# Making W' by Strassen over halves of in, rank and out, in blocks of 128 rows of in

## The chip, the cores and the metric

The kernel runs on one core of a Trainium2 chip. The metric is the device time of one execution in microseconds (us). The engines of the core are called as the profile calls them: PE (TensorE, matrix products), PEld (its weight loads), DVE (VectorE), ACT (ScalarE), POOL (GpSimd) and SP (SyncE, which here only issues DMAs). Each engine works through its own queue of instructions in order, and the engines wait for one another by semaphores.

## The reference, cut to what matters

All numbers are float32. The input x is 32 samples of 128 x 2048. The program has two layers, each of them a mixing of channels and a product:

```python
# layer 0
agg_w, agg_b = softmax(mlp(cond)) @ weight, ... @ bias_k   # a 128x128 kernel for each sample
c   = einsum('boi,bih->boh', agg_w, x) + agg_b
out = einsum('bsd,od->bso', c, W) + bias                   # W: 2048 x 2048
xa  = einsum('bsd,erd->ebsr', c, A)                        # A: 16 x 16 x 2048
upd = einsum('ebsr,eor,e->bso', xa, Bf, coeffs * scales)   # Bf: 16 x 2048 x 16
x   = x + out + upd
# layer 1
c   = conv1d(x, 9 taps, 4 groups) + context + bias
x   = x + per_head_ffn(c)                                  # 16 heads of 128 -> 512 (gelu) -> 128
```

What matters here is that `out + upd` is one product with W' = W + Bf (w A), a matrix of 2048 x 2048 (in by out, as it is kept) whose second term is of rank 16 x 16 = 256. The change concerns how that second term is computed and added, and how W' is cut into blocks.

## The kernel before

**The product with W'.** The mixing of channels is linear and is done on the other side, so the product is x times W', over 4096 rows, 2048 in and 2048 out. It is done by Strassen's scheme (in Winograd's form, with seven products) over halves of rows, in and out. The seven outer products are the `ROUNDS`, in the order P1, P2, P6, P7, P5, P3, P4. Each round goes through eight groups g of rows, so there are 56 steps. A step is one call of `multiply` (L265), which is again Strassen's scheme with seven inner products P1 to P7, each of four 128x512 matmuls. The left operands are combinations of a tile of x, made by `x_combine` (L222) on POOL; the right operands are combinations of four quarters of a half-by-half piece of W', made by `inner_weights` (L184). POOL also makes the outer combinations of x (`x_outer`, L245, lines 249 and 251), for rounds to come, and stores them (L209). Each product goes to a PSUM bank, from which ACT copies it (L276) or DVE adds it (L274) into the output tile. There are eight banks, handed out and given back in a first-in, first-out list (`bank`, `done`). SBUF has 24 large slots of 8 KB a partition (`slot`).

**Making W'.** W' has 16 blocks. In the kernel before a block is (kh, oh, ki, oi): a half kh of in and a half oh of out, and halves ki and oi within these; it holds 512 rows of in (as four pieces kc of 128) and 512 columns of out. `w_load` (L151) loads W's block, and `w_make` (L156) adds the low-rank part: for each kc two matmuls (rank is 2 x 128) into a bank (L165), an add by DVE onto the loaded block (L169), and at the end a store into HBM (L171), since later rounds read the blocks again. A and Bf lie in SBUF in two halves each (`a_sb`, `bf_sb`), loaded by `low_load` (L130) on SP, and A is scaled by coeffs x scales on DVE (`a_scale`, L134). The first four blocks are made before step 0, since they are the right operand of round P1. The other twelve are made two at a time ahead of each of steps 0 to 5 ("pairs" 0 to 5 here). The first round's inner weights are made on DVE (line 869); those of the other rounds are made on POOL (lines 188, 189, 193 and 194).

**Row sums.** The sum of W' over in is needed for a bias. `row_sums` (L173) reduces a block's four pieces by a tensor_reduce on DVE (lines 178 and 181) and adds the result to `wsum` (L179).

**Order.** `tc.manual_schedule()` keeps the order of the program, so an instruction's place in its engine's queue is the place where it is written. The main part (from L785) issues the loads on SP, then the four first blocks, then the steps. In a step, operands and loads of the step that follows come first, then the making of the two blocks, then `multiply`, and `between(j)` puts other work after the j-th inner product. PE's waits follow from banks (a bank is written again only when it was read), operands, and accumulation: a product that adds to a bank comes after the read of what the bank held.

Of the kernel before, what the change touches and what calls it, by code (L numbers as in the profile page):

```python
# [8 lines left out]
FP = mybir.dt.float32  # L9
# [7 lines left out]
P = 128  # L17
# [34 lines left out]
def adaln_ffn_kernel(  # L52
# [29 lines left out]
    def bank():  # L82
        return banks.pop(0)
# [4 lines left out]
    def scratch(name, shape=(P, L)):  # L88
        return dram.tile(list(shape), FP, name=name, tag=name)
# [3 lines left out]
    wb_d = {  # L93
        (kh, oh, ki, oi): scratch(f"wb_d{kh}{oh}{ki}{oi}")
        for kh in range(2) for oh in range(2) for ki in range(2) for oi in range(2)
    }
    t2_d = {(ki, oi): scratch(f"t2_d{ki}{oi}") for ki in range(2) for oi in range(2)}
    w1_d = scratch("w1_d")
# [23 lines left out]

    a_sb = [slot(f"a_sb{h}", (P, 2, L // 2)) for h in range(2)]
    bf_sb = [slot(f"bf_sb{h}", (P, 2, L // 2)) for h in range(2)]

    def low(ts, c, i0, n):
        h, i0 = divmod(i0, L // 2)
        return ts[h][:, c, i0 : i0 + n]

    def low_load(ts, src, i0, n):  # L130
        h, j0 = divmod(i0, L // 2)
        nc.sync.dma_start(ts[h][:, :, j0 : j0 + n], src[:, :, i0 : i0 + n])

    def a_scale(i0, n):  # L134
        for c in range(2):
            cols = low(a_sb, c, i0, n)
            nc.vector.tensor_scalar(cols, cols, wsc[:, c : c + 1], None, ALU.mult)

# [8 lines left out]

    wsum = slot("wsum", (P, NPH, QW))
    seen = set()

    def w_load(kh, oh, ki, oi):  # L151
        t = slot(f"w_{kh}{oh}{ki}{oi}", (P, 4, QW))
        nc.sync.dma_start(t.rearrange("p k o -> p (k o)"), WT[kh, oh, ki, oi])
        return t

    def w_make(t, kh, oh, ki, oi):  # L156
        o = 2 * oh + oi
        for kc in range(4):
            pw = bank()
            i0 = kh * 1024 + ki * 512 + kc * P  # L160

            n = QW // 2 if i0 == 0 and o == 0 else QW
            for o0 in range(0, QW, n):
                for c in range(2):
                    nc.tensor.matmul(  # L165
                        pw[:, o0 : o0 + n], lhsT=low(a_sb, c, i0, P),
                        rhs=low(bf_sb, c, o * QW + o0, n), start=(c == 0), stop=(c == 1),
                    )
            nc.vector.tensor_tensor(t[:, kc], pw, t[:, kc], ALU.add)  # L169
            done(pw)  # L170
        nc.gpsimd.dma_start(wb_d[kh, oh, ki, oi], t.rearrange("p k o -> p (k o)"))  # L171

    def row_sums(t, oh, oi):  # L173
        o = 2 * oh + oi
        ks = t.rearrange("p k o -> p o k")
        if o in seen:
            part = agp.tile([P, QW], FP, name=f"part_{len(seen)}", tag="cq", bufs=1)
            nc.vector.tensor_reduce(part, ks, AX.X, ALU.add)
            nc.vector.tensor_tensor(wsum[:, o], wsum[:, o], part, ALU.add)  # L179
        else:  # L180
            nc.vector.tensor_reduce(wsum[:, o], ks, AX.X, ALU.add)
        seen.add(o)

    def inner_weights(name, t, eng=nc.gpsimd):  # L184

        b11, b12, b21, b22 = (t[k] for k in ((0, 0), (0, 1), (1, 0), (1, 1)))
        t1, t2, t4 = (slot(f"{name}_t{k}", (P, 4, QW)) for k in (1, 2, 4))
        eng.tensor_tensor(t1, b12, b11, ALU.subtract)
        eng.tensor_tensor(t2, b22, t1, ALU.subtract)
        if eng is nc.vector:  # L190
            t["late"] = b12
        else:
            eng.tensor_tensor(b12, b22, b12, ALU.subtract)
        eng.tensor_tensor(t4, b21, t2, ALU.subtract)
        return {"P1": b11, "P2": b21, "P3": b22, "P4": t4, "P5": t1, "P6": t2, "P7": b12}

# [68 lines left out]
    def multiply(r, g, lhs, rhs, olds, between):  # L265
# [13 lines left out]
        def product(k, ps, first, last):  # L279
            for kc in range(4):  # L280
                nc.tensor.matmul(  # L281
                    ps, lhsT=lhs[k][:, bass.ts(kc, P)], rhs=rhs[k][:, kc],
                    start=first and kc == 0, stop=last and kc == 3, skip_group_check=True,
                )
# [26 lines left out]

    def outer_weights(r, ki, oi):

        def get(d):
            t = slot(f"wo_{r}{ki}{oi}", (P, 4, QW))
            nc.sync.dma_start(t.rearrange("p k o -> p (k o)"), d)
            return t

        def w(kh, oh):
            return wb_d[kh, oh, ki, oi]  # L320

        tt = nc.gpsimd.tensor_tensor
        srcs = {
            "P6": [w(1, 1), w(0, 1), w(0, 0)],
            "P7": [w(1, 1), w(0, 1)],
            "P5": [w(0, 1), w(0, 0)],
            "P4": [w(1, 0), t2_d[ki, oi]],
            "P3": [w(1, 1)],
        }[r]
        ts = [get(d) for d in srcs]  # L330

        def combine():
            if len(ts) > 1:
                tt(ts[0], ts[0], ts[1], ALU.subtract)
            if len(ts) > 2:
                tt(ts[0], ts[0], ts[2], ALU.add)
                nc.gpsimd.dma_start(t2_d[ki, oi], ts[0].rearrange("p k o -> p (k o)"))
            return ts[0]

        return combine  # L340
# [325 lines left out]
    def small():  # L666
# [81 lines left out]
        for o in range(NPH):  # L748
            p5 = bank()
            for half in (slice(0, NQ), slice(NQ, QW)):  # L750
                nc.tensor.matmul(
                    p5[:, half], lhsT=ones, rhs=wsum[:, o, half], start=True, stop=True
                )
            nc.scalar.copy(wbc[:, o], p5)
            done(p5)
# [31 lines left out]
    blocks = [  # L787
        (kh, oh, ki, oi)
        for kh, oh in ((0, 0), (0, 1), (1, 1), (1, 0)) for ki in range(2) for oi in range(2)
    ]  # L790
    first = {}
    warm_up()
    nc.sync.dma_start(cs, coeffs)
    low_load(a_sb, A, 0, P)
    low_load(bf_sb, BfT, 0, QW // 2)
    low_load(bf_sb, BfT, QW // 2, QW // 2)
    nc.vector.tensor_tensor(wsc, cs[:, 0:2], cs[:, 2:4], ALU.mult)
    a_scale(0, P)
    low_load(a_sb, A, P, QW - P)
    a_scale(P, QW - P)  # L800
    low_load(bf_sb, BfT, QW, QW)
    wt = {k: w_load(*k) for k in blocks[0:1]}
    wt[blocks[1]] = w_load(*blocks[1])
    low_load(a_sb, A, QW, QW)
    xs = {0: [x_load(0, 0, 0)]}
    for k in blocks[2:4]:
        wt[k] = w_load(*k)

    def make(k):
        t = wt.pop(k)  # L810
        w_make(t, *k)
        made.append(k)
        if len(made) > 4:
            row_sums(t, k[1], k[3])
        return t

    steps = [(r, g) for r in ROUNDS for g in range(NG)]
    for i0 in (1024, 1536):
        low_load(bf_sb, BfT, i0, QW)
    for k in blocks[4:6]:  # L820
        wt[k] = w_load(*k)
    for i0 in (1024, 1536):
        low_load(a_sb, A, i0, QW)
    xs[0] += [x_load(0, 1, 0), x_load(0, 1, 1)]
    lhs = {}
    for n, k in enumerate(blocks[0:4]):
        first[k[2:]] = make(k)
        if n == 0:
            a_scale(QW, QW)
        if n == 1:  # L830
            lhs[0] = x_combine(*steps[0], xs.pop(0))
    rhs = inner_weights("P1", first, nc.vector)
    for i0 in (1024, 1536):
        a_scale(i0, QW)
    unsummed = [(0, 0), (1, 0), (1, 1)]
    olds = {}
# [8 lines left out]
    for i, (r, g) in enumerate(steps):  # L845
# [14 lines left out]
        if g == NG - 1 and 0 < ri < len(ROUNDS) - 1:  # L860
            nxt = inner_weights(ROUNDS[ri + 1], nxt)

        if ri == 0:
            for k in blocks[4 + 2 * g : 6 + 2 * g]:
                t = make(k)
                if "late" in first:
                    b12 = first.pop("late")
                    row_sums(b12, 0, 1)
                    nc.vector.tensor_tensor(b12, first[1, 1], b12, ALU.subtract)
                if k[:2] == (1, 0):  # L870
                    nxt[k[2:]] = t
        elif ri + 1 < len(ROUNDS):
            for k, combine in waiting.items():
                nxt[k] = combine()
            waiting = {}
            if 2 <= g < 6:
                k = ((g - 2) // 2, (g - 2) % 2)
                waiting[k] = outer_weights(ROUNDS[ri + 1], *k)

# [10 lines left out]
        def between(j):  # L890
# [3 lines left out]
            if ri == 0 and j == 2:  # L894
                for k in blocks[6 + 2 * g : 8 + 2 * g]:
                    wt[k] = w_load(*k)
            if ri == 0 and j == 4 and unsummed:
                ki, oi = unsummed.pop(0)
                row_sums(first[ki, oi], 0, oi)
            if last_round:  # L900
# [17 lines left out]
        if g == NG - 1 and ri + 1 < len(ROUNDS):  # L918
            rhs = nxt if ri > 0 else inner_weights(ROUNDS[ri + 1], nxt)
            nxt = {}  # L920
# [84 lines left out]
```

## Time and profile before

| What | us |
|---|---|
| median of three runs | 2664.43 (2660.68 to 2664.87) |
| the profiled execution | 2658.77 |
| its span on the core | 2657.0 |
| PE busy | 2630.5 |
| DVE busy | 1369.3 |
| POOL busy | 1087.3 |
| ACT busy | 535.2 |
| pair 0 on PE | up to 49.62 |
| step 0 on PE | 49.62 to 73.66 |
| a pair later on (32 PE instructions) | 13.81 |
| a step later on (56 PE instructions) | 24.03 |
| POOL's first inner weights for round P2 begin | 310.98 |

In the profile's rows a group of instructions is named by its line, engine and operation, then the tile that is written and the tiles that are read, by the names in the program, then its shape and count. A timeline's row has the start and the length in us ahead of that, and behind it in brackets how long the engine had been idle before and what ended the idle time. A 128x512 matmul in float32 is two PE instructions. PE's ends are modelled, and consecutive rows can overlap by a fraction of a us.

### The profile page before, as it was taken

What the parts mean: (1) busy time and instruction counts of PE and PEld (TensorE: products, weight loads), DVE (VectorE), ACT (ScalarE), POOL (GpSimd) and SP (SyncE); (2) the same over time, 40 slices, a digit from 0 to 9 for tenths busy, and PEclk for the clock granted to TensorE, in tenths of its full rate; (3) what the DMA queues carried; (4) which work ended last, traced back from release to release, by engine and by line L of the source; (5) the groups of instructions that cost most, each with busy time, mean ns of one, the idle gap of its engine ahead of it and who ended that gap; (6) DMA issues with size and microseconds to landing.
All of it is one profiled execution on the core that took longest, in us unless ns stands there. A gap on an engine that the chain in (4) does not pass through costs nothing.

```text
span 2657.0 us, 19770 instructions
## 1 busy us (share of the span) xinstructions
PE 2630.5 (99%) x6504; PEld 1235.7 (47%) x6504; DVE 1369.3 (52%) x2132; ACT 535.2 (20%) x1103; POOL 1087.3 (41%) x665
## 2 busy tenths in 40 slices
PE   9999999999999999999999999999999999999998
PEld 4444444444444444444444455554445544455543
DVE  6645245233344355444366667666666666666610
ACT  0000100000000000000011144434444444444432
POOL 3544645523646422656232233343333333343222
PEclk9999999999999999999999999999999999999999
DMA  8875548455366457555666788777788777777532
GB/s 332 349 303 232 233 170 328 158 199 201 155 265 239 157 238 285 221 217 210 219 235 204 249 298 285 229 219 239 232 248 248 225 229 226 239 244 232 164 124 87
DMA packets 183333, 609.14 MB, mean 229 GB/s; under 512 B 16832, under 2 KB 87488, under 8 KB 138816
## 3 DMA queue, kind: packets, MB, share of 16 engines
q1 hardware_dynamic: 148656, 466.40, 49.7%
q0 software_dynamic: 34144, 140.53, 15.4%
q8 instruction: 52, 0.85, 0.1%
q10 hardware_dynamic: 432, 0.96, 0.1%
q14 instruction: 49, 0.40, 0.0%
HBM read 364.03 MB, written 210.24 MB: 216 GB/s over the span
## 4 chain that ended last, share of the span: by engine, by line
PE 91%; DVE 4%; DMA 3%; POOL 1%; issue 1%; SPq 0%; POOLq 0%; ACT 0%; DVEq 0%; ACTq 0%
PE bank L281 47%; PE bank L626 16%; PE bank L637 16%; PE bank L484 6%; PE bank L394 4%; PE bank L165 2%; DVE ags L356 2%; DMA bf_sb<-in_BfT 1%; DMA xt<-in_xT 1%; DVE va L464 0%; DVE vb L463 0%; DMA wb_d<-w 0%; DVE u L274 0%; DMA ws<-in_ffw 0%; DVE vb L466 0%
## 5 line engine op out<-in xcount | busy, mean ns | idle before, releaser
L626 PE MATMUL bank<-t,ws 128*128 128x512 f32 x1024 | 460.4, 592 | 0.5 <-DMA ws<-in_ffw 0.5
L637 PE MATMUL bank<-gl,ws 128*128 128x512 f32 x1024 | 460.2, 592 | 0.0
L629 ACT ACTIVATE gl<-bank 128x512 f32<-128x512 f32 x512 | 306.1, 598 | 446.6 <-PE bank L626 430.1
L281 PE MATMUL bank<-P_t,s_P 128*128 128x512 f32 x896 | 393.8, 592 | 1.3 <-ACT m_P L276 0.9
L274 DVE TENSOR_TENSOR u<-bank,u 128x512 f32<-128x512 f32 x280 | 187.3, 687 | 398.3 <-PE bank L281 389.2
L644 POOL DMA_INDIRECT out<-t,orow x128 | 152.2, 1189 | 564.5 <-DVE t L642 503.2
L637 PEld LDWEIGHTS bank<-gl,ws 128*128 128x128 f32 x1024 | 194.6, 190 | 233.0 <-issue 231.0
L626 PEld LDWEIGHTS bank<-t,ws 128*128 128x128 f32 x1024 | 194.4, 190 | 227.5 <-issue 219.7
L281 PE MATMUL bank<-wo_P,s_P 128*128 128x512 f32 x640 | 284.7, 596 | 4.4 <-DVE u L274 4.4
L281 PEld LDWEIGHTS bank<-P_t,s_P 128*128 128x128 f32 x896 | 170.1, 190 | 215.3 <-issue 214.8
L385 ACT ACTIVATE bank<-w,aggb 128x512 f32<-128x512 f32 x128 | 80.8, 684 | 892.2 <-DMA w<-w_d 874.1
L642 DVE TENSOR_TENSOR t<-bank,t 128x512 f32<-128x512 f32 x128 | 87.9, 687 | 319.0 <-PE bank L637 304.8
L377 POOL TENSOR_TENSOR x<-x,fb 128x1024 f32<-128x1024 f32 x64 | 155.9, 2454 | 228.3 <-DMA x<-in_x 150.5
L274 DVE TENSOR_TENSOR p<-bank,p 128x512 f32<-128x512 f32 x112 | 77.3, 690 | 241.7 <-PE bank L281 241.7
L281 PEld LDWEIGHTS bank<-wo_P,s_P 128*128 128x128 f32 x640 | 121.5, 191 | 159.6 <-issue 149.5
L356 DVE SCALAR_TENSOR_TENSOR ags<-mix,att_bc,ags 128x128 f32<-128x128 f32 x224 | 174.5, 779 | 4.5
L281 PE MATMUL bank<-wo_P,xt 128*128 128x512 f32 x384 | 169.0, 592 | 0.0
L610 POOL DMA_INDIRECT t<-hx_d,row x128 | 125.0, 977 | 55.5 <-issue 25.0
L232 POOL TENSOR_TENSOR s_P<-xt 128x512 f32<-128x512 f32 x40 | 52.2, 1306 | 229.5 <-DMA xt<-in_xT 221.7
L281 PE MATMUL bank<-P_t,xt 128*128 128x512 f32 x320 | 144.0, 592 | 0.1
L484 PE MATMUL bank<-va,tw_l 128*128 128x256 f32 x512 | 123.0, 381 | 7.3 <-DVE va L467 7.1
L484 PEld LDWEIGHTS bank<-va,tw_l 128*128 128x128 f32 x512 | 96.7, 190 | 50.1 <-issue 38.0
(136 smaller groups left out, 2811.2 us busy)
## 6 DMA issues: line engine op xcount, KB each, us to landing
xt<-in_xT SPq DMA_DIRECT2D x64, 1024.0 KB
u<-u_d SPq DMA_DIRECT2D x40, 1024.0 KB
wo_P<-wb_d SPq DMA_DIRECT2D x36, 1024.0 KB
u<-c_d SPq DMA_DIRECT2D x64, 512.0 KB
x<-in_x SPq DMA_DIRECT2D x32, 1024.0 KB
xg<-x SPq DMA_DIRECT2D x256, 128.0 KB
hx_d<-x1t SPq DMA_DIRECT2D x32, 1024.0 KB
hx_d<-ht SPq DMA_DIRECT2D x32, 1024.0 KB
```

The source lines that it names most:

```text
L274: nc.vector.tensor_tensor(to, ps, to, ALU.add)
L281: nc.tensor.matmul(ps, lhsT=lhs[k][:, bass.ts(kc, P)], rhs=rhs[k][:, kc], start=first and kc == 0, stop=last and kc == 3, skip_group_check ...
L356: nc.vector.scalar_tensor_tensor(ag, mix[:, k], att, ag, ALU.mult, ALU.add)
L377: nc.gpsimd.tensor_tensor(xt[:, f : f + 2], xt[:, f : f + 2], late["fb"][:, f : f + 2], ALU.add)
L394: nc.tensor.matmul(pm, lhsT=ag, rhs=u[:, f], start=False, stop=True, skip_group_check=True)
L484: nc.tensor.matmul(out, lhsT=w[:, 2 * i + r], rhs=rhs, start=first and r == 0, stop=last and r == 1, skip_group_check=True,)
L610: nc.gpsimd.indirect_dma_start(out=t.rearrange("p k t -> p (k t)"), out_offset=None, in_=hx_d[g].rearrange("l k t -> l (k t)"), in_offset= ...
L626: nc.tensor.matmul(pu, lhsT=w[:, m * P : (m + 1) * P], rhs=t[:, 0], start=True, stop=True)
L629: nc.scalar.activation(gl[m], pu, AF.Gelu)
L637: nc.tensor.matmul(pd, lhsT=w[:, (MC + m) * P : (MC + m + 1) * P], rhs=gl[m], start=(m == 0), stop=(m == MC - 1),)
L642: nc.vector.tensor_tensor(t[:, 1], pd, t[:, 1], ALU.add)
L644: nc.gpsimd.indirect_dma_start(out=out, out_offset=bass.IndirectOffsetOnAxis(ap=orow[:, g, h : h + 1], axis=0), in_=t[:, 1], in_offset=None,)
```

## The change

A block of W' becomes (kh, oh, kc): 128 rows of each half ki of a half of in, and both halves oi of a half of out; its tile is 128 x (ki, oi, 512). A block thus has all four quarters that Strassen's scheme combines, for 128 of 512 rows. The host lays out W accordingly.

- The first four blocks are made as before, by eight matmuls each (`w_make`). The inner weights of the first round are made for each of them as soon as it is there, 512 columns at a time, on DVE.
- The other twelve are made in pairs by the new `w_make_two`: the low-rank product is done by Strassen's scheme over halves of in (ki), rank (c) and out (oi), with seven matmuls a block. Each matmul accumulates into one of three banks of the block, and after each DVE adds the bank onto a quarter of the block. The combined operands come from `a_combine` and `b_combine`, and take four slots more.
- A's second half is loaded on SP behind the x tiles of step 0, by `a_load`, which also does the two scales on DVE; on DVE they stand behind `tb[1]`'s four subtractions and ahead of the adds of pair 0.
- `row_sums` is two adds of 128x1024 a block, after the first and the third inner product of a step; the first four blocks have theirs in step 0 behind pair 0 (one half) and after the fifth inner product of steps 0 to 3. `wsum` begins at zero.
- The inner weights of the later rounds are made on POOL in 16 pieces of 128x512 instead of four of 128x2048.

The diff, cut to its core:

```diff
-    def low_load(ts, src, i0, n):
-        h, j0 = divmod(i0, L // 2)
-        nc.sync.dma_start(ts[h][:, :, j0 : j0 + n], src[:, :, i0 : i0 + n])
-
-    def a_scale(i0, n):
+    def a_load(h, k0, k1):
+        for ki in range(2):
+            i0 = (2 * h + ki) * QW
+            nc.sync.dma_start(
+                a_sb[h][:, :, ki, k0:k1].rearrange("p c k i -> p c (k i)"),
+                A[:, :, i0 + k0 * P : i0 + k1 * P],
+            )
         for c in range(2):
-            cols = low(a_sb, c, i0, n)
+            cols = a_sb[h][:, c, :, k0:k1]
             nc.vector.tensor_scalar(cols, cols, wsc[:, c : c + 1], None, ALU.mult)
...
+    def a_combine(kh, tt):
+        s = slot(f"sa_{kh}", (P, 4, 4, P))
+        x11, x12, x21, x22 = (a_sb[kh][:, c, ki] for ki in range(2) for c in range(2))
+        tt(s[:, 0], x21, x22, ALU.add)
+        tt(s[:, 1], s[:, 0], x11, ALU.subtract)
+        tt(s[:, 2], x11, x21, ALU.subtract)
+        tt(s[:, 3], x12, s[:, 1], ALU.subtract)
...
+    def w_make_two(ks, ts, sa, tb):
+        pxs, pys, pzs = ([bank() for _ in ks] for _ in range(3))
+
+        def product(n, ps, first, last, ki, oi):
+            for (_, _, kc), p, t in zip(ks, ps, ts):
+                nc.tensor.matmul(
+                    p, lhsT=sa[n][:, kc], rhs=tb[n], start=first, stop=last, skip_group_check=True
+                )
+                nc.vector.tensor_tensor(t[:, ki, oi], p, t[:, ki, oi], ALU.add)
+
+        product("P1", pxs, True, False, 0, 0)
+        product("P2", pzs, True, True, 0, 0)
+        done(*pzs)
+        product("P6", pxs, False, False, 0, 1)
+        product("P5", pys, True, False, 1, 1)
+        product("P7", pxs, False, False, 1, 1)
+        product("P3", pys, False, True, 0, 1)
+        done(*pys)
+        product("P4", pxs, False, True, 1, 0)
+        done(*pxs)
...
-            nc.vector.tensor_reduce(part, ks, AX.X, ALU.add)
-            nc.vector.tensor_tensor(wsum[:, o], wsum[:, o], part, ALU.add)
...
+    def row_sums(oh, t):
+        for ki in range(2):
+            nc.vector.tensor_tensor(wsum[:, oh], wsum[:, oh], t[:, ki], ALU.add)
...
-        eng.tensor_tensor(t1, b12, b11, ALU.subtract)
-        eng.tensor_tensor(t2, b22, t1, ALU.subtract)
...
+        for kc, t in enumerate(ts):
+            b11, b12, b21, b22 = (t[:, ki, oi] for ki in range(2) for oi in range(2))
+            tt(t1[:, kc], b12, b11, ALU.subtract)
+            tt(t2[:, kc], b22, t1[:, kc], ALU.subtract)
+            tt(b12, b22, b12, ALU.subtract)
+            tt(t4[:, kc], b21, t2[:, kc], ALU.subtract)
...
+    a_load(0, 0, 1)
+    b_load(0, 0, 0, QW // 2)
+    b_load(0, 0, QW // 2, QW // 2)
+    b_load(0, 1)
+    a_load(0, 1, 4)
+    wt = {k: w_load(*k) for k in blocks[0:2]}
     xs = {0: [x_load(0, 0, 0)]}
     for k in blocks[2:4]:
         wt[k] = w_load(*k)
...
-    for i0 in (1024, 1536):
-        low_load(bf_sb, BfT, i0, QW)
+    for q in range(2):
+        b_load(1, q)
     for k in blocks[4:6]:
         wt[k] = w_load(*k)
-    for i0 in (1024, 1536):
-        low_load(a_sb, A, i0, QW)
     xs[0] += [x_load(0, 1, 0), x_load(0, 1, 1)]
...
+    for kc, t in enumerate(first):
+        k = blocks[kc]
+        w_make(k, t)
...
+        tt(t1[:, kc], t[:, 0, 1], t[:, 0, 0], ALU.subtract)
+        tt(t2[:, kc], t[:, 1, 1], t1[:, kc], ALU.subtract)
+        tt(t4[:, kc], t[:, 1, 0], t2[:, kc], ALU.subtract)
+    rhs = weights(first, t1, t2, t4)
+    tb[1] = b_combine(1, nc.vector.tensor_tensor)
+    a_load(1, 0, 4)
...
+                w_make_two(ks, two, sa[ks[0][0]], tb[ks[0][1]])
+                made.extend(ks)
+                if g == 0:
+                    for kc, t in enumerate(first):
+                        b12 = t[:, 0, 1]
+                        nc.vector.tensor_tensor(wsum[:, 0, 1], wsum[:, 0, 1], b12, ALU.add)
+                        nc.vector.tensor_tensor(b12, t[:, 1, 1], b12, ALU.subtract)
+                if g == 1:
+                    sa[1] = a_combine(1, nc.gpsimd.tensor_tensor)
+                if g == 3:
+                    tb[0] = b_combine(0, nc.gpsimd.tensor_tensor)
...
+            if ri == 0 and j in (1, 3) and unsummed:
+                row_sums(*unsummed.pop())
+            if ri == 0 and j == 5 and unsummed_first:
+                t = unsummed_first.pop(0)
+                tt = nc.vector.tensor_tensor
+                tt(wsum[:, 0, 0], wsum[:, 0, 0], t[:, 0, 0], ALU.add)
+                tt(wsum[:, 0], wsum[:, 0], t[:, 1], ALU.add)
```

`b_combine` does for Bf, over rank and out, what `a_combine` does for A.

## The prediction

> **What bounds the kernel now.** I read the busy times first: the time of this kernel is TensorE's time.
>
> ```profile
> span 2657.0 us, 19770 instructions
> PE 2630.5 (99%) x6504; PEld 1235.7 (47%) x6504; DVE 1369.3 (52%) x2132; ACT 535.2 (20%) x1103; POOL 1087.3 (41%) x665
> ```
>
> A matmul taken away saves its whole length, and a wait put on PE costs its whole length. The profiled execution took 2658.77 us, 5.66 below the median of the runs, 2664.43; I sum against the former and add 5.66 at the end. Next, PE's waits and the chain of waits in the stretch that the change touches:
>
> ```profile
> PE bank L145 <- DVE warm L142: 1.5, 1, 1.5
> PE bank L281 <- ACT m_P L276: 0.9, 1, 0.9
> PE bank L165 <- DMA bf_sb<-in_BfT: 0.8, 1, 0.8
> ```
>
> ```profile
> 112.84 13.81 PE bank L165 x32
> 126.66 24.03 PE bank L281 x56
> ```
>
> After the start PE waits once, 0.9 us, in the first 250 us. The chain alternates: 32 PE instructions for a pair of W' blocks, 13.81 us; 56 for a step, 24.03. A 128x512 matmul is two PE instructions, 13.81/16 = 0.86 us each.
>
> Then the timelines. Weight loads show PE's pace at the start:
>
> ```profile
> 2.48 0.34 PEld L145 LDWEIGHTS bank<-warm 128*128 128x128 f32 x1 [0.52 <-issue]
> 3.33 0.34 PEld L145 LDWEIGHTS bank<-warm 128*128 128x128 f32 x1 [0.52 <-issue]
> ...
> 11.00 0.19 PEld L165 LDWEIGHTS bank<-bf_sb,a_sb 128*128 128x128 f32 x1 [0.24 <-issue]
> 11.43 0.19 PEld L165 LDWEIGHTS bank<-bf_sb,a_sb 128*128 128x128 f32 x1 [0.24 <-issue]
> ```
>
> Start to start is 0.85 us cold and 0.43 later: PE begins at half pace. VectorE around pair 0 (PE: 35.9 to 49.62):
>
> ```profile
> 44.75 0.88 DVE L137 TENSOR_SCALAR a_sb<-a_sb,wsc 128x512 f32<-128x512 f32 x2 [1.12 <-DMA a_sb<-in_A]
> 46.06 0.88 DVE L137 TENSOR_SCALAR a_sb<-a_sb,wsc 128x512 f32<-128x512 f32 x2 [0.43 <-DMA a_sb<-in_A]
> 46.86 2.48 DVE L169 TENSOR_TENSOR w<-bank,w 128x512 f32<-128x512 f32 x4
> 49.37 7.36 DVE L181 TENSOR_REDUCE wsum<-w 128x512 f32<-128x2048 f32 x2
> 56.77 2.81 DVE L869 TENSOR_TENSOR w<-w,w 128x2048 f32<-128x2048 f32 x1
> ```
>
> The second half of A is scaled, as it lands, ahead of pair 0's adds in VectorE's queue. So those adds start at 46.86, 11 us after their matmuls did. PE did not notice: pair 0 needs eight banks, eight are there, and no matmul waits for an add. GpSimd gives the pace of the loads and a price of sharing:
>
> ```profile
> 53.58 1.27 POOL L232 TENSOR_TENSOR s_P<-xt 128x512 f32<-128x512 f32 x1 [15.96 <-DMA xt<-in_xT]
> ...
> 57.38 3.33 POOL L235 TENSOR_TENSOR s_P<-xt,s_P 128x512 f32<-128x512 f32 x1
> 60.67 4.54 POOL L249 TENSOR_TENSOR xt<-xt,xt 128x2048 f32<-128x2048 f32 x1
> ```
>
> Three 1 MB x tiles follow A on SP's queue; the last lands at 53.5, so (53.5 − 46.0)/3 = 2.5 us a tile. And L235, 1.27 alone, took 3.33 while VectorE's L869 ran. The reverse is seen later:
>
> ```profile
> 246.50 4.52 POOL L251 TENSOR_TENSOR xt<-xt,xt 128x2048 f32<-128x2048 f32 x1
> ```
>
> ```profile
> 247.46 4.12 DVE L179 TENSOR_TENSOR wsum<-wsum,part 128x512 f32<-128x512 f32 x1
> ...
> 85.17 0.69 DVE L179 TENSOR_TENSOR wsum<-wsum,part 128x512 f32<-128x512 f32 x1
> ```
>
> L179, 0.69 alone, took 4.12 and ended with GpSimd's operation: an SBUF-to-SBUF add of VectorE stands still while GpSimd adds. With a bank as operand (L169, 2.48 for four) no such stretch is seen.
>
> **The change part by part.**
>
> *Matmuls.* Each of six pairs has 14 instead of 16: −2 × 0.86 = −1.72; six pairs −10.3. PSUM adds go from 8 to 14 a pair (+6 × 0.69 on VectorE, half idle; hidden except where priced below). The wait of 0.9 us (step 1's output tile in a slot whose old content was being stored) goes, as the slots shift: −0.9 (0 to −0.9).
>
> *Start.* One more load stands on SP ahead of the first matmul (0.61 to 0.68 us of issue each in the chain), and eight instead of four half-width matmuls run at the slow start: +0.8 (0 to 1.5). Pair 0 starts at 36.7.
>
> *Pair 0: the new wait.* Its seven products share banks. P6 adds into the bank that P1 filled, so it waits until VectorE has added P1's to W'. Four matmuls (P1 and P2 of both blocks) can run: 36.7 + 3.4 = 40.1. The adds stand in VectorE's queue behind the scales of the second half of A, as before; those wait for the load, which the change also puts behind x tiles (0,1,0) and (0,1,1) on SP. It landed at 46.0; two tiles later is 51.0 (46 if queues overlap so that order doesn't matter; 53.5 if it lands where the third tile did; I take 51.0, from the tiles' pace). Two scales of 128x1024, 1.5, one add 0.7: P6 starts at 53.2, PE has stood 13.1 (8.2 to 15.6). Queued behind the same scales are all adds of pair 0, and behind them step 0's. After the stop PE starts cold: the first loads' pitch was 0.85 instead of 0.43 for about 4 us, +2.0 (0 if 13 us of rest don't cool it, 2.2 at the start's worst). Sum here +15.1; pair 0's own −1.72 is counted above.
>
> The Trainium skill, "TensorE: Matmul & The Clock Gate", Part 1 (the HAM clock gate), says that an idle window of some 3.4 us drops the array to half clock and a busy one of that length restores it; by it the restart loses an estimated 1.7 (3.4 at half pace) and the sum below would be +9.6 instead of +9.9. The profile's granted clock shows 1.00 in the first 10 us, where the pitch is 0.85; the pitch decides, and the column can't.
>
> *Step 0.* Behind pair 0's adds VectorE has eight new SBUF-to-SBUF adds (128x512: row sums of the first blocks, P7's weights), then per step four 128x1024 row sums in place of reductions (3.7). In step 0, about 64 to 88, GpSimd runs its four 4.5 us operations (x_outer; 60.7 to 81.4 before), with gaps of 0.9 us, and one or two of VectorE's fit a gap. Going gap by gap the P7 weights are done near 82, the row sums near 88, the P7 product's add at 88.6: P7 and P4 of step 0 wait 4.2 in all (0 if VectorE's run first in each gap and hold GpSimd instead; 8 if every one waits for an operation of 4.5). I take 4.2, from the two rows above. In steps 1 to 5 GpSimd mostly rests while these sums run: 0 (cover: PE's other products, 24 us a step; without it, up to 4 a step, rival C).
>
> *First-round weights* are subtracted by 512 columns as each block comes, 12 operations of 0.69 under 32 products of 27 us: hidden; before, three of 2.3 stood at the end with nothing waiting but P5 and P6. A's and Bf's combinations: sa_0 on GpSimd, 4 × 1.27 while x is loading; sa_1 and tb_0 (5 us each) a pair ahead of use on GpSimd, which is 41% busy: 0, at most 2. Stores to HBM and reloads keep size and count.
>
> *Round P2's start.* GpSimd makes its weights from 310.98, four operations of 4.5; the second, which P6 of step 8 needs at 324.5, ends at 320.0. In 16 pieces of 1.24 pitch the last piece of t2 comes at 310.98 + 17.4 = 328.4, and P6 reaches it at 324.5 + 3 × 0.86 = 327: +1.4 to +2.6. Against that, PE's 0.97 at 332.51, behind VectorE's L354 and L356 stretched to 2.7 and 4.5, can shrink. Net +1.0 (−1 to +3). In later rounds these weights end 5 us and more ahead of use: 0.
>
> Sum: −10.3 − 0.9 + 0.8 + 15.1 + 4.2 + 1.0 = +9.9. 2658.77 + 9.9 = 2668.7 profiled; **2674.3 as median**.
>
> **The rivals.** About 0.2%, 5.3 us, is what a measurement tells from no change.
> - A, the wait is there, the rest is not: no cold restart, no sharing price in step 0, or a load near 47 to 49. +2 to +6, about 2668. For it: L179 shows the sharing price in one place only. Against: L235 shows it in the other direction.
> - B, faster: the second half of A arrives before P6 needs it. Place: VectorE's first scale. The sum crosses zero when PE stands 13.1 − 9.9 = 3.2 or less, i.e. the load is there by about 41; without step 0's price and the cold start, by 47. With no wait at all −9.4: about 2655. Against it: in before, with less ahead of it, the load came at 46.0, and the queue is served in order as far as the arrivals show.
> - C, the price of sharing in every step of round P1: each block's row sums meet GpSimd's 4.5 us operations, 1 to 2 us a step over five steps: +15 to +20, about 2682. For: x_outer runs in each step. Against: its position in the step is late or early by 10 us, and PE has three banks of slack.
> - D, the pieces don't do less: Strassen's adds in PSUM put a wait in every pair (P6 after P1's add, P4 after P7's). Each add is 0.69, and three matmuls lie between a product and the next into its bank: 2.6 of cover, so it holds. If not, 0.7 × 3 a pair, +12 on top. Against: banks and adds as above.
>
> **How the numbers follow.** Main case 0.50 (2669 to 2679), A 0.22, C 0.16, D 0.03, B 0.09. The range reaches into A's and C's: 2664 to 2683; outside it lie B and the far ends of C and D. Faster than 2659.1: B, 0.08. Within 0.2% (to 2669.7): most of A and a little of B, 0.19. Slower: 0.73.
>
> **What would show it.** Right: one wait of PE of 8 to 16 us near 40, released by VectorE's add, which stands behind two scales that the load of A released; weight loads at 0.85 pitch behind it; pairs of 28 PE instructions in 12.1; VectorE adds of 4 us inside GpSimd's in step 0, and a wait of PE of 2 to 5 there; 1 to 3 us near 325. Wrong: the load of A landing by 41; step 0 in 24.0; waits in pairs 1 to 5, or stretched products there; any change behind round P2's start beyond 1 us.

## The result, and the profile after

The changed kernel takes 2673.39 us (median of 6 runs, 2670.64 to 2675.43), the kernel before 2662.55 (6 runs, 2660.18 to 2665.74). The ratio is 1.0039, 95% interval 1.0026 to 1.0052: 10.8 us slower. The profiled execution took 2672.8, its span is 2671.0 (before: 2657.0).

The page of the changed kernel, span and busy times:

```profile
span 2671.0 us, 19893 instructions
PE 2624.4 (98%) x6484; PEld 1233.8 (46%) x6484; DVE 1404.4 (53%) x2188; ACT 535.2 (20%) x1103; POOL 1117.0 (42%) x750
```

PE is busy for 6 us less and the span is 14 us longer: PE waits more. PE's waits up to 360 us (who waited, for whom; us in all, times, longest):

```profile
PE bank L208 <- DVE w L211: 13.6, 3, 12.8
PE bank L334 <- DVE w L917: 1.7, 3, 1.3
PE bank L334 <- DVE m_P L327: 1.6, 1, 1.6
PE bank L334 <- POOL P_t L237: 1.5, 1, 1.5
...
```

Each stands where it was looked for: pair 0 (L208), P7's weights and P4 in step 0 (L917, L327), round P2's start (L237). PE's timeline, from pair 0's stop to pair 1:

```profile
51.92 8.10 PE L208 MATMUL bank<-tb,sa 128*128 128x512 f32 x12 [12.83 <-DVE w L211]
...
63.29 7.03 PE L334 MATMUL bank<-w,xt 128*128 128x512 f32 x16
...
79.35 1.13 PE L334 MATMUL bank<-w,s_P 128*128 128x512 f32 x2 [1.31 <-DVE w L917]
...
88.12 3.70 PE L334 MATMUL bank<-P_t,xt 128*128 128x512 f32 x8 [1.55 <-DVE m_P L327]
91.66 3.60 PE L208 MATMUL bank<-bf_sb,a_sb 128*128 128x512 f32 x8
```

Step 0 begins at 63.29 (49.62 before) and ends at 91.66 (73.66 before). VectorE in the same stretch:

```profile
49.75 1.42 DVE L135 TENSOR_SCALAR a_sb<-a_sb,wsc 128x1024 f32<-128x1024 f32 x2 [8.79 <-DMA a_sb<-in_A]
51.09 2.48 DVE L211 TENSOR_TENSOR w<-bank,w 128x512 f32<-128x512 f32 x4
...
64.10 3.69 DVE L916 TENSOR_TENSOR wsum<-wsum,w 128x512 f32<-128x512 f32 x1
67.82 5.36 DVE L917 TENSOR_TENSOR w<-w 128x512 f32<-128x512 f32 x1
73.10 5.47 DVE L916 TENSOR_TENSOR wsum<-wsum,w 128x512 f32<-128x512 f32 x1
78.61 0.69 DVE L917 TENSOR_TENSOR w<-w 128x512 f32<-128x512 f32 x1
```

VectorE rests for 8.79 us until A's second half lands at 49.75; pair 0's adds follow. Then three adds of 0.69 take 3.7 to 5.5, until GpSimd is through; its rows:

```profile
62.71 4.52 POOL L304 TENSOR_TENSOR xt<-xt,xt 128x2048 f32<-128x2048 f32 x1
...
68.10 4.52 POOL L302 TENSOR_TENSOR xt<-xt,xt 128x2048 f32<-128x2048 f32 x1
...
73.50 4.52 POOL L304 TENSOR_TENSOR xt<-xt,xt 128x2048 f32<-128x2048 f32 x1
```

The adds end at 67.8, 73.1 and 78.6, each 0.6 behind the end of one of GpSimd's (67.2, 72.6, 78.0). And the pace of PE behind the stop, by its weight loads:

```profile
53.75 0.34 PEld L208 LDWEIGHTS bank<-tb,sa 128*128 128x128 f32 x1 [0.52 <-issue]
54.61 0.34 PEld L208 LDWEIGHTS bank<-tb,sa 128*128 128x128 f32 x1 [0.52 <-issue]
...
57.71 0.19 PEld L208 LDWEIGHTS bank<-tb,sa 128*128 128x128 f32 x1 [0.24 <-issue]
58.14 0.19 PEld L208 LDWEIGHTS bank<-tb,sa 128*128 128x128 f32 x1 [0.24 <-issue]
```

Start to start it is 0.86 up to 57.2 and 0.43 from 57.7 on. The profile's granted clock shows the same. In its rows by stretch it is the third number from the end (the last two are the DMA engines' share and GB/s):

```profile
43.00:45.00 2.00, 0.00 (x0) 0.00 (x0) 0.00 (x0) 0.00 (x0) 0.00 (x0) 0.68 1.03 436
45.00:57.00 12.00, 5.08 (x6) 2.18 (x7) 5.19 (x8) 0.00 (x0) 4.63 (x4) 0.50 0.92 372
57.00:58.00 1.00, 1.00 (x3) 0.49 (x2) 0.59 (x1) 0.00 (x0) 1.00 (x2) 0.81 0.00 0
```

It is 1.00 before 43 and from 58 on. By the shares it fell to half at 43.7, 4.6 us after PE had stopped, and came back at 57.4.

Against the kernel before, at the same work (PE's timelines): step 0 begins 13.7 later, ends 18.0 later; step 1 begins 16.3 later, step 2 13.5, step 3 11.7, step 4 10.4, step 5 10.1, round P2 10.1; at 720 us it is 10.0. The two profiled executions drift apart by 4 us more after 1160 us, in small waits. From round P2's start to the end it is 2339.4 in the kernel before and 2343.2 in the changed one, but 2337.7 in e2 below, which runs the same program there; so this part differs as much between executions. The medians differ by 10.8.

### The profile page after: what moved, and what is told of

Same layout as the page of the kernel before. It is cut to its first block, busy times and chain, and to the rows that moved or that the text cites. A ratio compares the mean times of both kernels' runs of the same rounds, so it can differ in the third digit from the quotient of the medians.

```text
span 2671.0 us, 19893 instructions
## 1 busy us (share of the span) xinstructions
PE 2624.4 (98%) x6484; PEld 1233.8 (46%) x6484; DVE 1404.4 (53%) x2188; ACT 535.2 (20%) x1103; POOL 1117.0 (42%) x750
## 4 chain that ended last, share of the span: by engine, by line
PE 90%; DVE 5%; DMA 2%; POOL 1%; issue 1%; SPq 0%; ACT 0%; POOLq 0%; DVEq 0%
PE bank L334 46%; PE bank L679 16%; PE bank L690 16%; PE bank L537 6%; PE bank L447 4%; PE bank L208 2%; DVE ags L409 2%; DMA a_sb<-in_A 1%; DMA w<-in_WT 1%; DVE u L327 0%; DMA xt<-in_xT 0%; DVE vb L519 0%; DVE wsum L916 0%; DMA ws<-in_ffw 0%; DVE vb L516 0%
## 5 line engine op out<-in xcount | busy, mean ns | idle before, releaser
L327 DVE TENSOR_TENSOR u<-bank,u 128x512 f32<-128x512 f32 x280 | 187.3, 687 | 387.4 <-PE bank L334 378.3
L327 DVE TENSOR_TENSOR p<-bank,p 128x512 f32<-128x512 f32 x112 | 77.4, 691 | 246.7 <-PE bank L334 244.9
L409 DVE SCALAR_TENSOR_TENSOR ags<-mix,att_bc,ags 128x128 f32<-128x128 f32 x224 | 182.9, 816 | 4.5
## 6 DMA issues: line engine op xcount, KB each, us to landing
u<-u_d SPq DMA_DIRECT2D x40, 1024.0 KB, 10.6
```

The source lines that it names most:

```text
L327: nc.vector.tensor_tensor(to, ps, to, ALU.add)
L409: nc.vector.scalar_tensor_tensor(ag, mix[:, k], att, ag, ALU.mult, ALU.add)
```

## The experiments

All twelve were timed against the kernel before on the same chip; its medians there were 2662.3 to 2663.7. "Ratio" is to that kernel, with its 95% interval.

| kernel | median us | ratio | step 0 begins / ends | round P2 begins |
|---|---|---|---|---|
| before | 2662.55 | | 49.62 / 73.66 | 317.64 |
| changed | 2673.39 | 1.0039 [1.0026, 1.0052] | 63.29 / 91.66 | 327.77 |
| e1_scale_late | 2672.96 | 1.0036 [1.0023, 1.0050] | 50.72 / 92.68 | 328.79 |
| e2_load_first | 2671.49 | 1.0037 [1.0024, 1.0050] | 58.87 / 91.50 | 327.61 |
| e3_plain_pairs | 2677.90 | 1.0057 [1.0042, 1.0073] | 53.28 / 92.58 | 335.45 |
| e4_keep_warm | 2674.65 | 1.0048 [1.0033, 1.0064] | 61.68 / 92.07 | 328.18 |
| e5_no_outer | 2667.23 | 1.0016 [1.0006, 1.0026] | 62.98 / 87.01 | 323.12 |
| e6_no_outer_late | 2667.30 | 1.0013 [1.0003, 1.0023] | 54.21 / 83.05 | 319.16 |
| e7_outer_later | 2694.10 | 1.0118 [1.0102, 1.0134] | 51.38 / 80.31 | 334.52 |
| e8_all | 2686.24 | 1.0089 [1.0075, 1.0103] | 51.60 / 83.13 | 338.05 |
| e9_three_gates | 2666.98 | 1.0016 [1.0007, 1.0026] | 50.85 / 74.89 | 323.22 |
| e10_t2_first | 2665.76 | 1.0014 [1.0004, 1.0025] | 51.11 / 75.15 | 323.54 |
| e11_no_gates | 2672.87 | 1.0043 [1.0029, 1.0058] | 51.54 / 75.57 | 327.08 |
| e12_sa_early | 2673.43 | 1.0036 [1.0023, 1.0050] | 50.74 / 74.77 | 328.29 |

**First round: the stop in pair 0.**

e1_scale_late takes the scales of A's second half out from ahead of pair 0's adds:

```diff
-    a_load(1, 0, 4)                       # two loads on SP, two scales on DVE
+    a_load(1, 0, 4)                       # the loads alone
...
                         nc.vector.tensor_tensor(b12, t[:, 1, 1], b12, ALU.subtract)
+                    a_scale(1, 0, 4)      # behind the last of these, once
```

> As the changed kernel, but the two scales of A's second half stand on VectorE behind pair 0's adds and the eight adds of step 0 (its load keeps its place on SP). My theory (pair 0's wait is VectorE's order, not the seven products): the wait of 12.8 us before P6 goes, with it the slow restart (2.8); pair 0 takes 12.1 and step 0 begins near 47.5 instead of 63.3, so -15.8; step 0's own waits of 4.3 shrink if VectorE's adds are through before GpSimd's 4.5 us operations begin at 57, else they stay. 2653 to 2658 against 2673 for the changed kernel and 2662.5 for the one before. Rival (the products' own order of banks makes the wait): P6 still waits, 2673.

Half right, and the missed half matters most. Pair 0's wait falls from 12.8 to 2.6 and step 0 begins at 50.7; the order on VectorE made the wait. But the median is 2672.96, and step 0 ends at 92.7. PE's rows of e1:

```profile
42.06 5.39 PE L210 MATMUL bank<-tb,sa 128*128 128x512 f32 x12 [2.62 <-DVE w L213]
...
72.44 10.10 PE L336 MATMUL bank<-P_t,s_P 128*128 128x512 f32 x16 [14.69 <-ACT m_P L331]
```

The step's P6 waits 14.69 us for ScalarE's first copy. ScalarE's rows, and GpSimd's:

```profile
70.51 1.28 ACT L331 ACT_TABLE_LOAD   x1 [70.51 <-DMA s_d<-xt]
71.81 0.59 ACT L331 COPY m_P<-bank 128x512 f32<-128x512 f32 x1
```

```profile
60.96 4.94 POOL L304 TENSOR_TENSOR xt<-xt,xt 128x2048 f32<-128x2048 f32 x1
66.20 0.56 POOL L264 DMA_DIRECT2D s_d<-xt  x1 [0.30 <-POOL xt L304]
```

ScalarE writes step 0's output tile. By the two slots that `sa_0` and `tb_1` take before it, that tile has no fresh slot left; it lies in x tile (0,1,0)'s (the late slot, below), which is free when GpSimd has added to the x tile (65.9) and the store of it has landed (70.5). In the changed kernel the same gate opens before step 0 needs it, since the stop in pair 0 comes first: ScalarE's first copy, at 66.96, waits for PE alone.

e2_load_first loads A's second half ahead of the two x tiles:

```diff
+    a_load(1, 0, 4)                       # the loads alone
     xs[0] += [x_load(0, 1, 0), x_load(0, 1, 1)]
...
-    a_load(1, 0, 4)
+    a_scale(1, 0, 4)
```

> As the changed kernel, but the loads of A's second half stand on SP ahead of the x tiles (0,1,0) and (0,1,1), as in the kernel before; the scales stay ahead of pair 0's adds. My theory (SP's queue is served in order, 2.5 us a tile): A lands 5 us earlier, about 44.7, P6's wait is 7.8 instead of 12.8, the slow restart (2.8) stays or shrinks, since 7.8 us of rest may or may not cool the array: -5 to -8, 2665 to 2668. GpSimd's combination of x comes no earlier. Rival (order on the queue hardly matters, loads share the engines): A lands within 1 us of 49.75, 2673.

A lands at 45.4 instead of 49.75, 4.4 for two tiles: the queue is served in order, at 2.2 a tile. The wait is 7.46 (forecast 7.8), and the slow pace stays. Step 0 begins 4.4 earlier, and then 3.05 go to the copy into the late slot and 1.8 to the slow pace behind that wait (P6 and P5 take 8.83 instead of 7.03), while P7's waits for its weights shrink by 0.7: it ends at 91.50, 0.2 earlier than in the changed kernel. The time, 2671.5, isn't told apart from the changed kernel's.

e3_plain_pairs makes the pairs without Strassen's scheme:

```diff
-                w_make_two(ks, two, sa[ks[0][0]], tb[ks[0][1]])
+                for k, t in zip(ks, two):
+                    w_make(k, t)
```

> As the changed kernel (blocks, loads, scales, combinations, row sums), but the pairs are made by 16 plain matmuls, each in its own bank, instead of 14 with Strassen's scheme. My theory: eight banks carry PE through pair 0, which ends near 49.3; only step 0's first product, which takes a bank again, waits for VectorE's first add (51.8), 2 to 3 us; so step 0 begins near 52 instead of 63.3, -11.3; five pairs cost 1.72 each more, +8.6; step 0's own waits of 4.3 stay or shrink by 1 to 2. Sum -3 to -5, about 2669. Rival (the wait belongs to the new loads and not to the products): pair 0 waits as long as now, 2673 + 10 = 2683.

Pair 0 runs through, as forecast, and step 0's first product waits (5.03, not 2 to 3). But the time is 2677.9, not 2669: what step 0 gained at its begin is again gone at its end (92.58). PE's row:

```profile
80.96 8.35 PE L334 MATMUL bank<-w,s_P 128*128 128x512 f32 x12 [9.65 <-DVE w L918]
```

P7 waits 9.65 us for its weights. ScalarE's first copy, at 58.49, waits for PE alone: it comes before GpSimd has begun to add to x tile (0,1,0) (59.22), so here, where no pair reads `sa_0` and `tb_1`, the output tile does not lie in that x tile's slot. That fits the reading of e1, and e9 below tests it. Round P2 begins 7.7 later than in the changed kernel: that is what Strassen's scheme saves up to there in this order of work (six pairs of 1.72 are 10.3; by the medians 4.5, with intervals that overlap).

e4_keep_warm fills the stop with matmuls that nobody reads:

```diff
         product("P2", pzs, True, True, 0, 0)
         done(*pzs)
+        pw = bank()
+        for _ in range(fill):             # 14 in pair 0, else 0
+            nc.tensor.matmul(pw, lhsT=sa["P1"][:, 0], rhs=tb["P1"], start=True, stop=True)
+        done(pw)
```

> As the changed kernel, with 14 more 128x512 matmuls (12.0 us, into a bank that nobody reads) between P2 and P6 of pair 0, where PE now rests for 12.8 us. My theory (the rest cools the array, the half pace behind it is its price): the weight loads behind the wait have a pitch of 0.43 from the first on, step 0 begins 2.8 us earlier, near 60.5; in all -1 to -3, about 2671. Rival (the half pace has to do with what P6 reads, or with the semaphore): the pitch of 0.85 stays, 2673.

PE's rows of e4:

```profile
53.02 5.39 PE L208 MATMUL bank<-tb,sa 128*128 128x512 f32 x12 [1.15 <-DVE w L211]
...
61.68 7.03 PE L338 MATMUL bank<-w,xt 128*128 128x512 f32 x16
...
79.76 1.13 PE L338 MATMUL bank<-w,s_P 128*128 128x512 f32 x2 [2.26 <-DVE w L921]
```

Twelve PE instructions behind the filled stop take 5.39 (8.10 in the changed kernel): the rest is what slows PE. The granted clock stays 1.00 from 39 to 58, where it fell to 0.50 in the changed kernel. Step 0 begins only 1.6 earlier, as pair 0's P6 begins 1.1 later; then 0.8 goes to the copy into the late slot, and P7's wait grows from 1.31 to 2.26: it ends at 92.07. No gain (2674.65).

So four kernels with step 0 begun at 50.7, 53.3, 58.9 and 61.7 all end it between 91.5 and 92.7. In e1 the copy into the late slot holds it, in e3 P7's weights, in e2 and e4 some of both. The first theory, that the stop in pair 0 costs its length, falls: something else holds step 0's end. New theory: it is GpSimd's four additions of x_outer, which hold the slot of the output tile and VectorE's adds behind them.

**Second round: GpSimd's additions.**

e5_no_outer and e6_no_outer_late leave the four additions out of the changed kernel and of e1:

```diff
+            if g > 1:
                 tt(b, b, c, ALU.add)
             part_store("s1", g, b)
+            if g > 1:
                 tt(c, b, a, ALU.subtract)
```

> As the changed kernel, but GpSimd leaves out the four adds of x_outer in step 0 (lines 302 and 304 for groups 0 and 1; their stores stay, so what later rounds read of these groups is not the combination). Theory one (in step 0 VectorE's SBUF adds stand still while GpSimd adds): the first adds of 0.69 are no longer 3.7 to 5.5, P7's weights are ready by 70, step 0 takes 24.0 instead of 28.3 and ends near 87.4 instead of 91.7. Theory two (VectorE has simply too many adds behind pair 0): the waits of P7 and P4 stay, 91.7.

> As e1_scale_late, with the same four adds of GpSimd left out. Theory (behind the removed wait of pair 0 stands a second gate: step 0's output tile lies, by the four new slots, in the slot of x tile (0,1,0), which is free when GpSimd has added to it and stored it): the store of (0,1,0) is issued near 60 and done near 64 instead of 70.5, so P6 of step 0 waits some 6 us instead of 14.7; the half pace behind it stays; step 0 ends near 84 instead of 92.7. Were the gate something else, it stays at 92.

Rows of e5, VectorE's, and then PE's of e6:

```profile
63.79 0.68 DVE L918 TENSOR_TENSOR wsum<-wsum,w 128x512 f32<-128x512 f32 x1
64.50 0.69 DVE L919 TENSOR_TENSOR w<-w 128x512 f32<-128x512 f32 x1
65.11 0.69 DVE L918 TENSOR_TENSOR wsum<-wsum,w 128x512 f32<-128x512 f32 x1
```

```profile
64.11 8.80 PE L338 MATMUL bank<-P_t,s_P 128*128 128x512 f32 x16 [2.87 <-ACT m_P L333]
...
83.05 3.60 PE L210 MATMUL bank<-bf_sb,a_sb 128*128 128x512 f32 x8
```

Both as the new theory has it. In e5 each add takes 0.69 again, step 0 takes 24.03 instead of 28.37, and the time falls by 6.2 (4.3 of it in step 0). In e6 the wait for the output tile is 2.87 instead of 14.69 (forecast 6), step 0 ends at 83.05 instead of 92.68 (forecast 84), and round P2 begins 8.6 earlier than in the changed kernel. Against e5 the trace of e6 is 4.0 ahead at round P2 and 5.9 at the end (spans 2661.1 and 2667.0); the medians are equal (2667.3 and 2667.2), and intervals of 2.7 us either way do not decide between the two.

**Third round: complete versions without the gates.**

These leave nothing out. In the code `between(j)` counts from 0: j = 1, 3 and 5 stand behind the second, fourth and sixth inner product, which the description of the change and several forecasts call the first, third and fifth.

e7_outer_later and e8_all load group g+1's second and third x tile late in step g, and add them up a step later; e8 also moves weights:

```diff
-            "P1": lambda: [x_load(g, 0, 0), x_load(g, 1, 0), x_load(g, 1, 1)],
+            "P1": lambda: [x_load(g, 0, 0)],
...
+            if ri == 0 and j == 5 and i == 0:
+                a_scale(1, 0, 4)
+            if ri == 0 and j == 5 and g + 1 < NG:
+                outer.append((g + 1, [tail.pop(), x_load(g + 1, 1, 0), x_load(g + 1, 1, 1)]))
```

> A complete version: as the changed kernel, but the scales of A's second half stand after the fifth product of step 0, and the second and third x tile of the next group are loaded after the fifth product of a step (not at its start) and added up by x_outer one step later. That frees two slots when step 0's output tile is taken, and GpSimd has two operations of 4.5 us in step 0 instead of four. Theory (VectorE's order, the slot, and GpSimd's adds are the three gates, one behind the other): pair 0 waits 2.6 for VectorE, step 0 begins near 50.7 and ends at 75 to 77 instead of 91.7: -15 to -17, 2656 to 2659, 4 to 6 below the kernel before. If a fourth gate stands behind (loads that now come later, rounds' later slots), step 1 or 2 gives part of it back: 2660 to 2668.

> As e7_outer_later, and two small ones: the last of the first blocks has its inner weights made behind pair 0's adds instead of ahead (pair 0's wait of 2.6 shrinks to 0.5), and GpSimd makes t1 and t2 of all four pieces first in a round's inner weights (the wait of 1.5 at round P2's start goes). -2 to -4 against e7_outer_later: 2653 to 2657.

Both wrong, 2694.1 and 2686.2. Step 0 does end 11.4 earlier (80.31; P7 still waits 2.8), but the stages behind it pay: step 4 begins 4.5 later than in the changed kernel, and round P2 6.8. PE's waits over the whole of e7, first the pairs, then round P2:

```profile
PE bank L210 <- DVE w L213: 10.5, 4, 5.4
...
PE bank L338 <- POOL P_t L239: 9.4, 3, 3.4
```

Row sums now meet GpSimd's additions while the next pair waits for VectorE, and the last x_outer stands on GpSimd ahead of round P2's inner weights. In e8 the moved weights leave 0.57 and 2.37 of pair 0's wait of 2.6. Its order of t2 removes the 9.4, but in step 7 P6 then waits 6.8 for ScalarE's copy into the output tile.

e9_three_gates and e10_t2_first keep the loads and clear step 0 alone:

```diff
-        t = slot("warm", (P, QW))
+        t = wsum[:, 0, 0]
...
+    m0 = [slot("m_P10", (P, 2, 2, QW))]          # taken ahead of group 1's x tiles
...
+            if i == 0:
+                x_outer()                        # ahead of x_combine for step 1
...
-            if ri == 0 and j in (1, 3) and unsummed:
+            if ri == 0 and j in ((1, 3) if g else (5,)):     # in step 0 both blocks
...
-                        nc.vector.tensor_tensor(wsum[:, 0, 1], wsum[:, 0, 1], b12, ALU.add)
+                tt(wsum[:, 0, 1], wsum[:, 0, 1], t[:, 1, 1], ALU.add)        # later, for b12
+                tt(wsum[:, 0, 1], wsum[:, 0, 1], t[:, 0, 1], ALU.subtract)
```

> A complete version that keeps the changed kernel's loads and x_outer from step 1 on and takes the three gates out of step 0: (1) the scales of A's second half stand after step 0's second product; (2) step 0's output tile takes a fresh slot (one slot is saved by using the row sums' tile for the warm-up, and x_outer of group 0 goes ahead of the combination of group 1's x, whose result takes the slot that it frees); (3) behind pair 0 VectorE has four adds for P7 instead of eight, the row sums of pair 0 stand after the fifth product of step 0, and those of the first blocks one step later with two adds more. Theory: pair 0 waits 2.6, step 0 begins near 50.7 and ends at 75 to 76, pair 1 waits 1 to 4 (row sums of pair 0 ahead of its adds; its second block of W loads into a slot that x_outer of group 1 frees near 72); step 1 begins at 88 to 91 instead of 103.7: -13 to -15, 2658 to 2660, 2 to 5 below the kernel before. Rival, as in e7_outer_later: what is gained in step 0 is lost to later slots and shared SBUF adds by round P2: 2664 or more.

> As e9_three_gates, and GpSimd makes t1 and t2 of all four pieces first, then the rest, in a round's inner weights: t2 is complete 4 operations of 1.24 earlier, so the wait of 1.5 at the start of round P2 goes: -1.5 against e9_three_gates (within the noise of the medians, so read by the wait in the trace). Rival: GpSimd starts these weights late because x tiles come late (its combination of x ended at 321 in the changed kernel, 311 in the one before), and the wait moves to t4 or to x: no change.

In e9 step 0 is clean: 50.85 to 74.89, 24.04. With a fresh slot for the output tile ScalarE's first copy comes at 54.53 and waits for PE alone. The 16.8 gained at its end are 9.9 at step 1's begin (pair 1 waits 3.3 for VectorE and restarts slowly), 7.4 at step 3's, 4.5 at step 4's (waits of 1.8 for VectorE in steps 2 and 3, of 1.0 in pair 4). The times are 2667.0 and 2665.8: 6 to 8 faster than the changed kernel, and still 1.0016 and 1.0014 of the kernel before. In e10 round P2's wait of 1.4 is gone, as forecast.

e11_no_gates and e12_sa_early go after those waits. e11 loads pair 1's W tiles into the last fresh slots and moves x_outer of group 1 into step 1; e12 then makes `sa[1]` on GpSimd ahead of the combination of x:

```diff
+            if i == 0:                           # e11
+                for k in blocks[6:8]:
+                    wt[k] = w_load(*k)
...
+            if i == 1:                           # e12
+                sa[1] = a_combine(1, nc.gpsimd.tensor_tensor)
```

> A complete version, from e10_t2_first, against the two waits that were left: pair 1's W tiles are loaded ahead of group 1's second and third x tile and take the last fresh slots (those two x tiles come after the third product of step 0, and x_outer of group 1 moves into step 1); the row sums of a step's pair stand after the first product (in step 0 after the second, both blocks) instead of after the first and third, so that they are through before P7's add is due. Theory (the waits of 3.3 and their slow restart in pair 1 come from row sums behind GpSimd's operations and from a tile that waits for a slot; those of 1.8 in steps 2 and 3 from row sums that meet x_outer): step 0 50.9 to 75, pair 1 to 87, steps 1 to 3 without waits over 0.5; round P2 begins near 311 to 315 (317.6 in the kernel before, 323.2 in e9_three_gates): 2654 to 2660, faster than both. Rival (each slot or adding time moved makes another late): 2663 or more.

> As e11_no_gates, with its two waits undone: A's second combination is made on GpSimd ahead of the combination of group 2's x (GpSimd rested there from 92 to 102), and the row sums of the first blocks stand in steps 2, 4 and 5 (not in steps 1 and 3, where they met x_outer and Bf's combination). Theory: pair 2 no longer waits for GpSimd (6.9, and its slow restart), pair 4 no longer 3.8; step 1 begins near 87.5, step 5 near 236 to 240 instead of 251.5 (242.1 in the kernel before), so -11 to -15 against e11_no_gates: 2656 to 2662, at or below the kernel before. Rival: another slot or addition is late in its turn, and step 5 begins past 244: 2664 or more.

The rivals were right both times. In e11 pair 1 is clean and step 1 begins at 87.59 (before: 87.39), but pair 2 waits, in PE's row:

```profile
122.37 2.08 PE L210 MATMUL bank<-tb,sa 128*128 128x512 f32 x2 [6.93 <-POOL sa L185]
```

In e12 that wait is gone, and another stands in the same pair. Rows of e12, of PE, of VectorE and of SP's queue:

```profile
129.53 6.51 PE L210 MATMUL bank<-tb,sa 128*128 128x512 f32 x10 [14.03 <-DVE w L213]
```

```profile
128.78 2.48 DVE L213 TENSOR_TENSOR w<-bank,w 128x512 f32<-128x512 f32 x4 [15.99 <-DMA w<-in_WT]
```

```profile
91.75 30.63 SPq L156 DMA_DIRECT2D w<-in_WT  x2
```

SP's queue stands 30.63 us at the loads of two W tiles: the slot that the second is to take is freed by x_outer of group 2 on GpSimd, which the earlier `sa[1]` pushed back from 107.5 to 112.1. No version tried beats the kernel before.

## Why the prediction was right, and where it wasn't

The forecast was +9.9 (2674.3; range 2664 to 2683), the medians say +10.8, the traces +10.0 to 10.7 up to 720 us. Step by step, in us:

| step of the sum | forecast | measured |
|---|---|---|
| start | +0.8 | −0.3 (pair 0 at 35.5; before 49.62 − 13.81 = 35.8) |
| A lands | 51.0 | 49.75 |
| PE stands in pair 0 | 13.1 | 12.8 |
| restart | +2.0 | +2.8 (63.29 − 51.92 = 11.37 for ten matmuls of 0.858) |
| step 0 | +4.2 | +4.3 (28.37 against 24.04) |
| fewer matmuls | −10.3 | −8.5 |
| ScalarE's wait | −0.9 | −1.1 (step 1: 24.04 against 25.15) |
| round P2's start | +1.0 | +0.6 |
| sum | +9.9 | +10.6 |

The matmuls gave −1.72 in each of pairs 0 to 3. Pairs 4 and 5 gave 1.3 and 0.3 only: their P6 waits 0.2 and 0.6 for VectorE, and PE 0.3 for `ctxb`. The forecast held that pairs 1 to 5 would have no waits; for these two it was wrong by 1.8 in all.

The four waits stood where they were forecast, and released by what was forecast. In step 0 P7's weights were done at 81.95 (forecast 82), the row sums at 87.5 (88), and P7's product was added by 88.0 (88.6). How close the sum came is in part luck: its terms miss by −1.1 (start) to +1.8 (matmuls), and the misses cancel to +0.7. Of the signs of being wrong two appeared: the waits in pairs 4 and 5, and a change behind round P2's start beyond 1 us (3.9 between these two executions), which e2's 2337.7 puts within the differences between executions.

The sum is right, and its reading as a sum of independent prices is not. Two sentences of the prediction fail by the runs:

- Rival B's reckoning: "The sum crosses zero [...] the load is there by about 41; without step 0's price and the cold start, by 47." e1 takes the load out of the way altogether and gains 0.4 (not distinguishable from none), e2 brings it to 45.4 and gains 0.2 at step 0's end. The stop of 12.8 and its restart lie in parallel to a second gate, GpSimd's x_outer, that ends step 0 at about 92 in any case. The prices of pair 0 and of step 0 can't be undone one by one.
- "A's and Bf's combinations: [...] 0, at most 2." The additions cost nothing, as said, but the slots that their results take do: two of them stand ahead of step 0's output tile, which moves it from a fresh slot to one that GpSimd frees at 70.5 in e1 (14.69 of wait). The prediction named the shift of the slots only as a gain, for the wait of 0.9.

The price of sharing SBUF was taken from two rows (L235 at 3.33, L179 at 4.12) and is shown by e5: without GpSimd's additions step 0 is back at 24.03. Rival A's point against it, that L179 shows the price in one place only, misreads the kernel before: L179 also took 2.81 at 110.33 and 2.34 at 169.27, and ended each time 0.6 behind one of GpSimd's additions. The cold restart is shown by e4. It cost 2.8 and not the 1.7 estimated from the page, since PE worked at half clock for 5.5 us (51.9 to 57.4) and not for 3.4. The prediction held that the column of the granted clock can't show the pace; that is so in the first 10 us, and not at the stop, where it reads 0.50.

The Trainium skill's page "SBUF — State Buffer", section "SBUF: two separate sides", names the lock of the port pair that VectorE and GpSimd share as exclusive, and as binding VectorE when it has two SBUF inputs. The runs agree, and show the other side too: before, L181's reduction of one SBUF operand took 3.75 beside GpSimd's 4.5 us additions and 3.68 ahead of them, while the adds that the change puts in its place take up to 5.5 for 0.69.

## What to carry to other kernels

When a wait is found in front of a stage, look for what the stage would wait for next before pricing its removal: start the stage at several times by experiment, and if it always ends at the same time, the bound is elsewhere. A tile more in a full set of slots is a price, even if it is never late itself: it moves every later tile into a slot that someone else must free. In place of a one-operand reduction, two-operand adds in SBUF are not cheaper when GpSimd adds at the same time: the row to read is the same add beside GpSimd's operations and alone.

## What the runs showed of the hardware that was not expected

- A wait of 2.62 or 2.63 us in the same place of pair 0 left PE at full pace in six kernels (twelve PE instructions behind it took 5.39 in e1, e7, e9, e10, e11 and e12) and slowed it in another (6.96 in e6). Whether a rest of this length slows PE is thus not fixed by its length. The granted clock stays 1.00 in e1 from 39 to 49; in e6 it is 0.87 in 43 to 44, 0.50 in 44 to 47 and 0.92 in 47 to 48, so it fell at 43.7, just ahead of P6, and came back at 47.2. These 3.4 us at half clock, the 10.2 of e2 (42.7 to 52.9) and the 13.7 of the changed kernel (43.7 to 57.4) are one, three and four times the same length. A wait of 12.8 and one of 7.5 were each followed by about 5.5 us at half pace. The Trainium skill, "TensorE: Matmul & The Clock Gate", Part 1, has the activity window run freely, so that the point of change depends on where the work falls in it; that fits these steps of 3.4 us, though no run here shows by what share of work in a window the clock is set.
- The begin of pair 0 varied from 34.4 to 37.8 between profiled executions (e5 and e6) of kernels whose instructions up to there do the same work. A forecast of the start to better than 1 to 2 us can't be tested by single executions.
- Two tiles of 1 MB ahead in SP's queue cost 4.4 us (49.75 against 45.4 in e2), 2.2 a tile, where the arrivals of the kernel before gave 2.5.
